# First mixer, last phase: outputs with channels on partitions, head norm by sums over partitions, scores in 64-row pairs

## The chip, the cores and the metric

The kernel runs on one core of a Trainium2 chip. The metric is device time in microseconds (us). Three runs of the kernel before took 4608.09, 4599.14 and 4606.88 us, so the median is 4606.88 us. The engines are named as in the profile: PE is TensorE (PEld its weight loads), DVE is VectorE, ACT is ScalarE, POOL is GpSimd, SP is SyncE, which here issues most of the DMAs.

## The reference

The program is a stack of four pairs of a mixer and a feed-forward part over 8 sequences of 512 tokens and 256 channels. The change lies in the first mixer alone, a gated delta rule with 4 heads of 64 channels. Cut to what matters, with `F` the gated sum of three causal filters of the values and a direct term, and `g` a gate of the head's path, which the kernel multiplies into the queries ahead of time:

```python
def step(S, inp):                       # one chunk of tokens of one head
    q_i, k_i, u_i, w_i = inp
    attn = where(causal, q_i @ k_i.T, 0.0)
    u_adj = u_i - w_i @ S
    o_i = q_i @ S + attn @ u_adj
    return S + k_i.T @ u_adj, o_i
o = g * delta_rule(q, k, v, beta) + F   # 64 channels per head
o = o * rsqrt(mean(o * o, -1) + 1e-5)   # norm over the 64 channels of a head
y = (o * norm_w) @ Wo.T                 # then a layer norm, added to x
```

The reference scans over chunks of 32 tokens; the kernel works with chunks of 128, which gives the same result.

## The kernel before

The first mixer, `l0_attn` (from L275), has three parts. The first makes queries, keys and values of each of the 8 sequences ("batches" below), their products and the inverses of the 64x64 triangles. The second (the filters, L511 to L640) makes the filter term with Toeplitz matrices: L610 multiplies in pairs of 64 output rows, `pf`, with every eighth element of `toep` as the moving operand. Both leave their results in DRAM. The third, from L644, is the phase that the change touches. It loads everything back per batch and runs the recurrence, the outputs, the head norm and the projection.

`loads(b)` (L671) issues the loads of one batch on SP's queue, in the order TT (two halves of the transposed inverse, L677), T1 (two blocks of 32 columns of the inverse, L682), TS (L686 and L689), keys, queries, PQ, V and F (L704). POOL then scales the queries (L707). The loads of a batch are issued when the batch before it begins, except that those of the first two stand at the start.

`back(b, ...)` (L710) is a generator. It first joins 64x64 inverses into 128x128 ones: `pW` (L719, 32x32 products of T1 and TT), `pX` (L728 and L731), `pU` and `pV` (L743 and L751, 64 output rows). Then it takes four chunks `n` of 128 tokens. For every second chunk it makes the scores of two chunks: ACT copies the two heads of a channel pair into a tile QP with zeros in the other half (L766), PE multiplies the keys with it over all 128 rows and 256 columns (`pa`, L773), DVE masks (L778). For each chunk: `pk` transposes the keys (L784), `pr` is keys times state (L791), R = V - pr (DVE, L795), `pu` (L799), u (DVE, L803), `pS` (L809), the new state (DVE, L816 or L818), and the outputs `po`: the filter term times the identity (L823), queries times state (L826), scores times u (L828), one sum in PSUM with tokens on partitions. ACT copies it (L832) and squares it (L834), DVE sums the squares (L835). After the four chunks: the reciprocal root by a shift and three Newton steps on DVE (L94 to L96, of 16 values per partition), the scaling on POOL (L841), eight transposes to channels on partitions (`poT`, L847), two ACT copies (L850), and the projection `py` (L193) with the closing norm (`stats`, L99; ACT scales, L177; POOL adds to X, L182).

Two batches are interleaved by the loop at the end of `l0_attn`: one generator step of each in turn, a new batch when fewer than two are live and the last has made 8 steps. A planner then orders the instructions of each engine by costs and dependences, so that PE's order differs from that of the program. PSUM tiles of the tag `mm` have 3 buffers, `seq` 3 and `st` 2. An fp32 product appears as two records on PE in the trace, a transpose as one.

Of the kernel before, what the change touches and what calls it, by code (L numbers as in the profile page):

```python
# [19 lines left out]
P = 128  # L20
NB = 8
L = 512
NT = 4
# [251 lines left out]
def l0_attn(K):  # L275
# [6 lines left out]
    with ExitStack() as es:  # L282
# [17 lines left out]
        def window(t, offset, *ap):  # L300
            a = t[0:1, 0:1]
            return bass.AP(tensor=a.tensor, offset=a.offset + offset, ap=[list(x) for x in ap])
# [350 lines left out]
        QPs, Us = [], []  # L653
        T1s = [p1.tile([P, NT, H, 32], F32, name=f"T1{i}") for i in range(2)]
        W21s = [p1.tile([P, NT, H, 32], F32, name=f"W21{i}") for i in range(2)]
        for i in range(2):
            t = p1.tile([P, 2, 2, 2, P], F32, name=f"QP{i}")
            nc.gpsimd.memset(t, 0.0)
            QPs.append(t)
            t = p1.tile([P, 2, H, 64], F32, name=f"U{i}")  # L660
            nc.gpsimd.memset(t, 0.0)
            Us.append(t)
# [8 lines left out]
        def loads(b):  # L671
# [9 lines left out]
            for r in range(2):  # L681
                nc.sync.dma_start(  # L682
                    out=T1s[b % 2][64 * r:64 * r + 32].rearrange("p n h t -> p (n h) t"),
                    in_=window(t_d, (b * 32 + r * 16) * 4096,
                               (64, 32), (4096, NT * H), (1, 32)))
# [24 lines left out]
        def back(b, TT, TS, qT, kT, V, F):  # L710
# [6 lines left out]
            for n, h in heads:  # L717
                for r in range(2):
                    nc.tensor.matmul(  # L719
                        ps[two[r], n, h, :], lhsT=TT[one[r], n, h, two[r]],  # L720
                        rhs=T1[one[r], n, h, :], start=True, stop=True)
# [34 lines left out]
            O = p1.tile([P, NT, H, 64], F32, tag="O", name=f"O{b}", bufs=2)  # L756
            os_ = p2.tile([P, NT, H], F32, tag="os", name=f"os{b}")
            S = None
            for n in range(NT):
                u_ = f"{b}_{n}"  # L760
                tok = slice(n * P, (n + 1) * P)
                if n % 2 == 0:
                    QP = QPs[b % 2]
                    for r in range(2):
                        half = slice(64 * r, 64 * r + 64)
                        nc.scalar.copy(  # L766
                            QP[half, :, :, r, :],
                            qT[half, :, n * P:(n + 2) * P].rearrange("p c (m t) -> p c m t", m=2))
                    att = p2.tile([P, 2, H, P], F32, tag="at", name="at" + u_)
                    for m in range(2):  # L770
                        pa = pmm.tile([P, H, P], F32, tag="mm", name=f"pa{m}_" + u_)
                        for c in range(2):
                            nc.tensor.matmul(  # L773
                                pa[:, 2 * c:2 * c + 2, :].rearrange("p h t -> p (h t)"),
                                lhsT=kT[:, c, (n + m) * P:(n + m + 1) * P],
                                rhs=QP[:, c, m].rearrange("p r t -> p (r t)"),
                                start=True, stop=True)
                        nc.vector.tensor_tensor(  # L778
                            att[:, m], pa, K.up[:, None, :].to_broadcast([P, H, P]), ALU.mult)
# [40 lines left out]
                po = pseq.tile([P, H, 64], F32, tag="seq", name="po" + u_)  # L820
                for c in range(2):
                    pc = po[:, 2 * c:2 * c + 2, :].rearrange("p h d -> p (h d)")
                    nc.tensor.matmul(  # L823
                        pc, lhsT=F[:, c, tok], rhs=K.ident, start=(c == 0), stop=False)
                    if n > 0:
                        nc.tensor.matmul(pc, lhsT=qT[:, c, tok], rhs=S[:, c, :], start=False, stop=False)  # L826
                    for h in range(2 * c, 2 * c + 2):
                        nc.tensor.matmul(  # L828
                            po[:, h, :], lhsT=at[:, h, :], rhs=u[:, 64 * h:64 * h + 64],
                            start=False, stop=(h == H - 1))  # L830
                S = Sn
                nc.scalar.copy(O[:, n], po)  # L832
                oq = p2.tile([P, H, 64], F32, tag="oq", name="oq" + u_)
                nc.scalar.activation(oq, po, AF.Square)  # L834
                nc.vector.tensor_reduce(os_[:, n, :], oq, AX.X, ALU.add)  # L835
                yield

            nc.vector.tensor_scalar(os_, os_, 1.0 / 64, 1e-5, ALU.mult, ALU.add)
            ro = K.rsqrt(os_.rearrange("p n h -> p (n h)"), NT * H, "rms", p2)
            ro = ro.rearrange("p (n h) -> p n h", n=NT)  # L840
            nc.gpsimd.tensor_tensor(  # L841
                O, O, ro[:, :, :, None].to_broadcast([P, NT, H, 64]), ALU.mult)
            oT = p1.tile([P, 2, L], F32, tag="oT", name=f"oT{b}")
            for c in range(2):
                ps = pmm.tile([P, L], F32, tag="mm", name=f"poT{b}_{c}")
                for n in range(NT):
                    nc.tensor.transpose(  # L847
                        ps[:, n * P:(n + 1) * P],
                        O[:, n, 2 * c:2 * c + 2].rearrange("p h d -> p (h d)"), K.ident)
                nc.scalar.copy(oT[:, c, :], ps)  # L850
            K.project_out(b, [(oT[:, c, :], wo[:, c, :]) for c in range(2)], pmm, "mm", p1)


        ahead = {b: loads(b) for b in range(2)}
# [18 lines left out]

# [1738 lines left out]
```

## Time and profile before

| | |
|---|---|
| profiled execution, its own time | 4604.57 us |
| its span | 4602.9 us |
| median of three runs | 4606.88 us |
| mean granted PE clock | 0.926 |
| changed phase, first `pW` to the first product of the next part | 408.2 to 733.4 us |
| PE, busy in 408 to 733 | 273.4 of 325 us |
| DVE, ACT, POOL, busy in 408 to 733 | 145.0, 104.7, 56.2 us |

The span is cut into windows for the views below: each line of a window view has the busy time and number of instructions of each engine, the mean granted clock of PE, and the DMAs' share. In the views by line a group has its busy time, the mean duration of one in ns, and the idle time of its engine just ahead of it with what ended it. In the timeline a merged line has the start, the length from the first start to the last end, and the number of records.

### The profile page before, as it was taken

The page shows a single profiled execution, that of the slowest core. Times are in us where ns is not written, and L with a number is a line of the kernel's source. Part 1 is how long each engine was busy: PE and PEld are TensorE (multiplying, and loading weights), DVE is VectorE, ACT ScalarE, POOL GpSimd, SP SyncE. Part 2 cuts the span into 40 slices and gives each one's busy share as a digit, 9 for nine tenths or more (in the row PEclk, how much of TensorE's full clock was granted, in tenths as well). Part 3 has the DMA queues.
Part 4 walks back from the last instruction along what each step waited for, and adds up shares of the span by engine and source line. Part 5 has one row for each costly group of instructions (what it writes and reads, how often), then busy time and mean ns, then how long its engine had stood idle before and what let it go on. Part 6 is the DMA issues. An engine that isn't in the chain of part 4 may idle for free. (4 is left out here: it accounts for less than half of the span.)

```text
span 4602.9 us, 63430 instructions
## 1 busy us (share of the span) xinstructions
PE 3998.6 (87%) x21704; PEld 2678.3 (58%) x21704; DVE 2704.0 (59%) x7367; ACT 1984.7 (43%) x4096; POOL 2037.1 (44%) x2004
## 2 busy tenths in 40 slices
PE   8887888899998599789999987888888876799997
PEld 3434775555565389744455543556555545578884
DVE  7695546347657711145556533889888899731115
ACT  5512333344433333424444444677767656311112
POOL 0001111444433344344555412889888879223321
PEclk9898899999999899879999998989999986899999
DMA  4468430100000189700000001443333334237753
GB/s 120 132 200 231 101 72 15 48 5 11 5 7 16 46 212 251 192 5 6 10 6 6 1 23 48 122 127 128 120 122 127 122 108 138 93 124 227 233 182 112
DMA packets 393586, 443.42 MB, mean 96 GB/s; under 512 B 151693, under 2 KB 275711, under 8 KB 392751
## 3 DMA queue, kind: packets, MB, share of 16 engines
q1 hardware_dynamic: 365311, 390.70, 28.7%
q0 software_dynamic: 16272, 31.87, 2.5%
q10 hardware_dynamic: 11680, 16.80, 1.1%
q8 instruction: 172, 2.82, 0.3%
q14 instruction: 151, 1.24, 0.1%
HBM read 373.02 MB, written 66.26 MB: 95 GB/s over the span
## 5 line engine op out<-in xcount | busy, mean ns | idle before, releaser
L2027 POOL TENSOR_TENSOR h<-h,C 128x1024 f32<-128x1024 f32 x256 | 613.6, 2410 | 135.2 <-DVE h L2023 91.1
L2023 DVE TENSOR_TENSOR_SCAN h<-dA,dB 128x512 f32<-128x512 f32 x480 | 568.5, 1209 | 89.6 <-ACT dA L2011 73.3
L981 POOL TENSOR_SCALAR p<-p,rs 128x128 f32<-128x128 f32 (+3 forms) x256 | 275.7, 1085 | 420.7 <-DVE rs L980 263.1
L2011 ACT ACTIVATE dA<-dl,A 128x512 f32<-128x512 f32 x480 | 330.4, 690 | 174.1 <-DVE h L2023 173.3
L1547 DVE CUSTOM_DVE_ANT_0 junk<-S,mask 128x256 f32<-128x256 f32 (+3 forms) x512 | 249.7, 488 | 194.9 <-PE S L1541 156.3
L2040 PE MATMUL y<-C,h 128*128 128x128 f32 x2048 | 298.3, 297 | 68.0 <-POOL h L2027 67.9
L2040 PEld LDWEIGHTS y<-C,h 128*128 128x128 f32 x2048 | 263.4, 155 | 155.2 <-POOL h L2027 98.6
L1575 ACT ACTIVATE PT<-T 128x128 f32<-128x128 f32 (+3 forms) x512 | 198.1, 435 | 279.2 <-PE T L1570 268.3
L1541 PE MATMUL S<-KZ,QT 64*128 64x512 f32 (+3 forms) x1024 | 259.7, 489 | 23.5 <-DVE mx L1547 23.3
L2239 PE MATMUL gb<-xbT,w_b 128*128 128x256 f32 (+1 forms) x1472 | 255.3, 332 | 1.0 <-ACT ts L2443 0.6
L2239 PEld LDWEIGHTS gb<-xbT,w_b 128*128 128x128 f32 x1472 | 230.2, 191 | 23.1 <-ACT ts L2443 0.8
L2245 DVE TENSOR_TENSOR hTb<-sb,gb 128x512 f32<-128x512 f32 x71 | 48.8, 687 | 325.4 <-PE gb L2239 325.4
L2006 POOL TENSOR_TENSOR dB<-du,B 128x1024 f32<-128x1024 f32 x96 | 234.0, 2438 | 0.1
L1825 PE MATMUL pf<-fT,w_l_ffn 128*128 128x512 f32 x384 | 210.3, 687 | 26.2 <-ACT fT L1819 10.4
L1570 PE MATMUL T<-QT,KZ 64*128 64x384 f32 (+3 forms) x1024 | 217.1, 465 | 2.9 <-ACT PT L1575 2.5
L2006 DVE TENSOR_TENSOR dB<-du,pb 128x1024 f32<-128x1024 f32 x160 | 191.2, 1195 | 23.2 <-ACT pb L2004 21.3
L1315 ACT ACTIVATE hT<-h,w_l_ffn 128x128 f32<-128x128 f32 x384 | 109.5, 368 | 198.0 <-PE h L1310 198.0
L182 POOL TENSOR_TENSOR X<-X,yn 128x256 f32<-128x256 f32 (+1 forms) x56 | 79.3, 1434 | 260.2 <-ACT yn L177 230.2
L1310 PE MATMUL h<-xgT,w 128*128 128x128 f32 x1536 | 185.2, 279 | 0.0
L1541 PEld LDWEIGHTS S<-KZ,QT 64*128 64x128 f32 x1024 | 116.6, 192 | 114.0 <-issue 58.7
L979 ACT ACTIVATE p<-p,nm 128x128 f32<-128x128 f32 (+3 forms) x256 | 143.5, 561 | 81.1 <-DVE nm L975 73.1
L1578 POOL TENSOR_SCALAR_AFFINE_SELECT PT<-PT 128x512 f32<-128x512 f32 x128 | 81.3, 635 | 219.4 <-ACT PT L1575 206.5
(579 smaller groups left out, 9191.3 us busy)
## 6 DMA issues: line engine op xcount, KB each, us to landing
w_b<-l3f_w SPq DMA_DIRECT2D x138, 512.0 KB
C<-xdd SPq DMA_DIRECT2D x256, 256.0 KB
B<-xdd SPq DMA_DIRECT2D x256, 256.0 KB
w<-l1f_w SPq DMA_DIRECT2D x48, 1024.0 KB
w<-l1f_w SPq DMA_DIRECT2D x48, 256.0 KB
toep<-l0fd SPq DMA_DIRECT2D x32, 320.0 KB
X<-x SPq DMA_DIRECT2D x16, 512.0 KB
toep<-l0fd SPq DMA_DIRECT2D x32, 256.0 KB
```

What stands on the lines that cost most here:

```text
L981: nc.gpsimd.tensor_scalar(p[:, 0:n], p[:, 0:n], rs, None, ALU.mult)
L1541: nc.tensor.matmul(ps[:, 0:n], lhsT=QT[half, qt * P:n], rhs=KZ[half, j % 2, 0:n], start=True, stop=True)
L1547: nc.vector.tensor_tensor_reduce(out=junk[:, 0:n], in0=ps[:, 0:n], in1=mask[:, L - n:L], scale=1.0, scalar=-3.0e38, op0=ALU.add, op1=ALU.m ...
L1570: nc.tensor.matmul(ps[:, 0:n], lhsT=KZ[half, j % 2, kt * P:(kt + 1) * P], rhs=QT[half, kt * P:L], start=True, stop=True)
L1575: nc.scalar.activation(PT[:, j, :], ps[:, 0:n], AF.Exp)
L1825: nc.tensor.matmul(ps, lhsT=gu[:, k, j * 768 + c * P:j * 768 + (c + 1) * P], rhs=R[b]["fT"][:, k, :], start=(k == 0), stop=(k == 1))
L2006: on.tensor_tensor(dBs[k], R[b]["du", h], B[:, None, :].to_broadcast([P, 2, L]), ALU.mult)
L2011: nc.scalar.activation(dA, R[b]["dl", h][:, c, :], AF.Exp, scale=A[:, 2 * h + c, n:n + 1])
L2023: nc.vector.tensor_tensor_scan(hs[k][:, c, :], dA, dBs[k][:, c, :], 0.0, ALU.mult, ALU.add)
L2027: nc.gpsimd.tensor_tensor(hs[k], hs[k], row_C.pop(k)[:, None, :].to_broadcast([P, 2, L]), ALU.mult)
L2040: nc.tensor.matmul(R[b]["y", h][q // 2][:, q % 2, c * P:(c + 1) * P], lhsT=t[:, c, q * P:(q + 1) * P], rhs=K.ident, is_transpose=True, sta ...
L2239: nc.tensor.matmul(ps[:, q, :], lhsT=ww[:, k, (c + q) * P:(c + q + 1) * P], rhs=xT[:, k, :], start=(k == 0), stop=(k == 1))
```

## The change

Outputs are made transposed. `po` has channels on partitions (two chunks of 128 channels) and tokens along the row: queries times state with the state as the stationary operand, and scores times u as products with 64 output rows, the two heads of a chunk one above the other. The filter term, which lies in DRAM with channels on partitions already, is added by DVE when it takes `po` out of PSUM. ACT squares the sum. After the four chunks a product with a block matrix of 1/64 (`ones2`, `pss`) gives each channel its head's mean square; ACT makes the reciprocal root from Ln and Exp, DVE makes one Newton step from it, and POOL and DVE scale. The copies, the transposes and the row sums of before are gone. The end of a batch has two steps more in the generator.

The scores are made without QP: keys and queries of a head are multiplied over its 64 rows, for the two heads of a channel pair in turn, into two PSUM tiles. DVE masks each.

`pW` reads the first block of the inverse from TS, so that only one block of T1 is loaded.

The closing norm of the batches takes the branch with Ln and Exp in `stats` (L108) for this phase, and their table is loaded ahead of the phase.

```diff
--- before.py
+++ after.py
@@ -650,13 +650,15 @@
             t = p1.tile([P, NT, H, P], F32, name=f"TT{i}")
             nc.gpsimd.memset(t[64:128, :, :, 0:64], 0.0)
             TTs.append(t)
-        QPs, Us = [], []
+        Us = []
+        ones2 = p1.tile([P, P], F32, name="ones2")
+        nc.gpsimd.memset(ones2, 0.0)
+        for r in range(2):
+            half = slice(64 * r, 64 * r + 64)
+            nc.gpsimd.memset(ones2[half, half], 1.0 / 64)
         T1s = [p1.tile([P, NT, H, 32], F32, name=f"T1{i}") for i in range(2)]
         W21s = [p1.tile([P, NT, H, 32], F32, name=f"W21{i}") for i in range(2)]
         for i in range(2):
-            t = p1.tile([P, 2, 2, 2, P], F32, name=f"QP{i}")
-            nc.gpsimd.memset(t, 0.0)
-            QPs.append(t)
             t = p1.tile([P, 2, H, 64], F32, name=f"U{i}")
             nc.gpsimd.memset(t, 0.0)
             Us.append(t)
@@ -678,11 +680,9 @@
                     out=TT[half, :, :, half].rearrange("p n h t -> p (n h) t"),
                     in_=window(tt_d, (b * 32 + r * 16) * 4096,
                                (64, 64), (4096, NT * H), (1, 64)))
-            for r in range(2):
-                nc.sync.dma_start(
-                    out=T1s[b % 2][64 * r:64 * r + 32].rearrange("p n h t -> p (n h) t"),
-                    in_=window(t_d, (b * 32 + r * 16) * 4096,
-                               (64, 32), (4096, NT * H), (1, 32)))
+            nc.sync.dma_start(
+                out=T1s[b % 2][64:96].rearrange("p n h t -> p (n h) t"),
+                in_=window(t_d, (b * 32 + 16) * 4096, (64, 32), (4096, NT * H), (1, 32)))
             nc.sync.dma_start(
                 out=TS[0:64].rearrange("p n h t -> p (n h) t"),
                 in_=window(t_d, b * 32 * 4096, (64, 64), (4096, NT * H), (1, 64)))
@@ -718,7 +718,7 @@
                 for r in range(2):
                     nc.tensor.matmul(
                         ps[two[r], n, h, :], lhsT=TT[one[r], n, h, two[r]],
-                        rhs=T1[one[r], n, h, :], start=True, stop=True)
+                        rhs=(T1 if r else TS)[one[r], n, h, 0:32], start=True, stop=True)
             nc.scalar.copy(W21[two[0]], ps[two[0]])
             nc.vector.tensor_copy(W21[two[1]], ps[two[1]])
             yield
@@ -753,30 +753,28 @@
                             rhs=U[:, n, h, :], start=True, stop=True)
                 nc.scalar.mul(TT[0:64, ns, :, 64:128], ps, -1.0)
                 yield
-            O = p1.tile([P, NT, H, 64], F32, tag="O", name=f"O{b}", bufs=2)
-            os_ = p2.tile([P, NT, H], F32, tag="os", name=f"os{b}")
+            oT = p1.tile([P, 2, L], F32, tag="oT", name=f"oT{b}", bufs=2)
+            sq = p1.tile([P, 2, L], F32, tag="sq", name=f"sq{b}", bufs=2)
             S = None
             for n in range(NT):
                 u_ = f"{b}_{n}"
                 tok = slice(n * P, (n + 1) * P)
                 if n % 2 == 0:
-                    QP = QPs[b % 2]
+                    att = p2.tile([P, 2, H, P], F32, tag="at", name="at" + u_)
+                    pss = [pmm.tile([P, 2, 2, P], F32, tag="mm", name=f"pa{r}_" + u_)
+                           for r in range(2)]
+                    for m in range(2):
+                        to = slice((n + m) * P, (n + m + 1) * P)
+                        for c in range(2):
+                            for r in range(2):
+                                half = slice(64 * r, 64 * r + 64)
+                                nc.tensor.matmul(
+                                    pss[r][:, m, c, :], lhsT=kT[half, c, to],
+                                    rhs=qT[half, c, to], start=True, stop=True)
                     for r in range(2):
-                        half = slice(64 * r, 64 * r + 64)
-                        nc.scalar.copy(
-                            QP[half, :, :, r, :],
-                            qT[half, :, n * P:(n + 2) * P].rearrange("p c (m t) -> p c m t", m=2))
-                    att = p2.tile([P, 2, H, P], F32, tag="at", name="at" + u_)
-                    for m in range(2):
-                        pa = pmm.tile([P, H, P], F32, tag="mm", name=f"pa{m}_" + u_)
-                        for c in range(2):
-                            nc.tensor.matmul(
-                                pa[:, 2 * c:2 * c + 2, :].rearrange("p h t -> p (h t)"),
-                                lhsT=kT[:, c, (n + m) * P:(n + m + 1) * P],
-                                rhs=QP[:, c, m].rearrange("p r t -> p (r t)"),
-                                start=True, stop=True)
                         nc.vector.tensor_tensor(
-                            att[:, m], pa, K.up[:, None, :].to_broadcast([P, H, P]), ALU.mult)
+                            att[:, :, r::2, :], pss[r],
+                            K.up[:, None, None, :].to_broadcast([P, 2, 2, P]), ALU.mult)
                 at = att[:, n % 2]
                 if n < NT - 1:
                     pk = pmm.tile([P, D], F32, tag="mm", name="pk" + u_)
@@ -817,40 +815,41 @@
                         else:
                             nc.vector.tensor_tensor(
                                 Sn[half, :, half], S[half, :, half], pS[half, :, half], ALU.add)
-                po = pseq.tile([P, H, 64], F32, tag="seq", name="po" + u_)
+                po = pseq.tile([P, 2, P], F32, tag="seq", name="po" + u_)
                 for c in range(2):
-                    pc = po[:, 2 * c:2 * c + 2, :].rearrange("p h d -> p (h d)")
-                    nc.tensor.matmul(
-                        pc, lhsT=F[:, c, tok], rhs=K.ident, start=(c == 0), stop=False)
                     if n > 0:
-                        nc.tensor.matmul(pc, lhsT=qT[:, c, tok], rhs=S[:, c, :], start=False, stop=False)
-                    for h in range(2 * c, 2 * c + 2):
                         nc.tensor.matmul(
-                            po[:, h, :], lhsT=at[:, h, :], rhs=u[:, 64 * h:64 * h + 64],
-                            start=False, stop=(h == H - 1))
+                            po[:, c, :], lhsT=S[:, c, :], rhs=qT[:, c, tok], start=True, stop=False)
+                    for r in range(2):
+                        h = 2 * c + r
+                        nc.tensor.matmul(
+                            po[64 * r:64 * r + 64, c, :], lhsT=u[:, 64 * h:64 * h + 64],
+                            rhs=at[:, h, :], start=(n == 0), stop=True)
                 S = Sn
-                nc.scalar.copy(O[:, n], po)
-                oq = p2.tile([P, H, 64], F32, tag="oq", name="oq" + u_)
-                nc.scalar.activation(oq, po, AF.Square)
-                nc.vector.tensor_reduce(os_[:, n, :], oq, AX.X, ALU.add)
+                nc.vector.tensor_tensor(oT[:, :, tok], F[:, :, tok], po, ALU.add)
+                nc.scalar.activation(sq[:, :, tok], oT[:, :, tok], AF.Square)
                 yield
 
-            nc.vector.tensor_scalar(os_, os_, 1.0 / 64, 1e-5, ALU.mult, ALU.add)
-            ro = K.rsqrt(os_.rearrange("p n h -> p (n h)"), NT * H, "rms", p2)
-            ro = ro.rearrange("p (n h) -> p n h", n=NT)
-            nc.gpsimd.tensor_tensor(
-                O, O, ro[:, :, :, None].to_broadcast([P, NT, H, 64]), ALU.mult)
-            oT = p1.tile([P, 2, L], F32, tag="oT", name=f"oT{b}")
+            ro = p1.tile([P, 2, L], F32, tag="ro", name=f"ro{b}")
             for c in range(2):
-                ps = pmm.tile([P, L], F32, tag="mm", name=f"poT{b}_{c}")
-                for n in range(NT):
-                    nc.tensor.transpose(
-                        ps[:, n * P:(n + 1) * P],
-                        O[:, n, 2 * c:2 * c + 2].rearrange("p h d -> p (h d)"), K.ident)
-                nc.scalar.copy(oT[:, c, :], ps)
+                ps = pmm.tile([P, L], F32, tag="mm", name=f"pss{b}_{c}")
+                nc.tensor.matmul(ps, lhsT=ones2, rhs=sq[:, c, :], start=True, stop=True)
+                nc.scalar.activation(sq[:, c, :], ps, AF.Identity, bias=K.eps)
+                nc.scalar.activation(ro[:, c, :], sq[:, c, :], AF.Ln)
+            yield
+            for c in range(2):
+                nc.scalar.activation(ro[:, c, :], ro[:, c, :], AF.Exp, scale=-0.5)
+                t, y, o = sq[:, c, :], ro[:, c, :], oT[:, c, :]
+                nc.gpsimd.tensor_tensor(o, o, y, ALU.mult)
+                nc.vector.tensor_tensor(t, t, y, ALU.mult)
+                nc.vector.scalar_tensor_tensor(t, t, -0.5, y, ALU.mult, ALU.mult)
+                nc.vector.scalar_tensor_tensor(o, t, 1.5, o, ALU.add, ALU.mult)
+            yield
             K.project_out(b, [(oT[:, c, :], wo[:, c, :]) for c in range(2)], pmm, "mm", p1)
 
 
+        K.log_exp_tables()
+        K.log_exp = True
         ahead = {b: loads(b) for b in range(2)}
         live, done, begun, steps = [back(0, *ahead[0])], 0, 1, 0
         while live:
@@ -870,7 +869,7 @@
                     K.load_x(K.i["x"], range(HALF, NB))
                 if begun < NB:
                     ahead[begun] = loads(begun)
-
+        K.log_exp = False
 
 
 def l0_ffn(K):
```

## The prediction

> **What bounds the kernel now.** I read the page's busy times first, then cut the changed phase (408 to 733 us) into windows, then asked for its groups by shape, and last for the timeline and for the waits of PE and SP. The page:
>
> ```profile
> PE 3998.6 (87%) x21704; PEld 2678.3 (58%) x21704; DVE 2704.0 (59%) x7367; ACT 1984.7 (43%) x4096; POOL 2037.1 (44%) x2004
> ```
>
> The windows of the phase (engines in the order PE, PEld, DVE, ACT, POOL; then the granted clock):
>
> ```profile
> 408.00:433.00 25.00, 20.17 (x260) 18.20 (x260) 3.46 (x6) 7.08 (x13) 3.62 (x3) 0.53 0.96 218
> 555.00:630.00 75.00, 66.30 (x777) 58.63 (x772) 37.31 (x141) 27.53 (x58) 15.00 (x8) 0.91 0.49 102
> 630.00:705.00 75.00, 66.30 (x773) 58.92 (x772) 35.22 (x124) 25.06 (x54) 10.81 (x5) 0.91 0.09 22
> 705.00:733.00 28.00, 14.44 (x79) 11.58 (x77) 12.83 (x61) 6.28 (x15) 4.25 (x2) 0.85 0.15 53
> ```
>
> Two batches take 75 us in the steady part, and PE is busy in 66.3 of them; DVE fills half, ACT a third. So PE sets the pace, at an unsteady clock, and the price of the change is PE's time plus what PE waits for. At both ends of the phase one batch is alone and its chain sets the pace. The groups that the change removes or recasts, in the phase:
>
> ```profile
> L773 PE MATMUL pa<-QP,bk 128*128 128x256 f32 x128 | 44.7, 494 | 7.6 <-DVE W L723 3.6 <-DVE at L778 3.3 <-ACT QP L766 0.7
> L828 PE MATMUL po<-u,at 128*128 128x64 f32 x256 | 37.1, 269 | 0.1
> L823 PE MATMUL po<-C,bf 128*128 128x128 f32 x128 | 28.7, 307 | 0.0
> L847 PE MATMUL poT<-C,O 128*128 128x128 f32 x64 | 10.4, 314 | 11.9 <-POOL O L841 11.9
> ```
>
> Their durations overlap in the pipeline, so I price by starts. In the timeline at full clock, the start of each merged line less that of the one before is what a group costs PE; the other parts show products of 64 rows (`pkk`) and of 64 output rows (`pf`):
>
> ```profile
> 574.58 1.99 PE L773 MATMUL pa<-QP,bk 128*128 128x256 f32 x8
> 576.41 0.38 PE L784 MATMUL pk<-C,bk 128*128 128x128 f32 x2
> ...
> 577.25 0.44 PE L823 MATMUL po<-C,bf 128*128 128x128 f32 x2
> 577.52 0.39 PE L826 MATMUL po<-state,bq 128*128 128x128 f32 x2
> 577.75 0.56 PE L828 MATMUL po<-u,at 128*128 128x64 f32 x4
> 578.14 0.66 PE L809 MATMUL pS<-u,kt 128*128 128x128 f32 x4
> ```
> ```profile
> 42.71 0.27 PE L473 MATMUL pvw<-C,vT 128*128 128x128 f32 x1
> 42.92 1.60 PE L486 MATMUL pkk<-kT 64*128 64x128 f32 x22
> 44.45 0.33 PE L146 MATMUL pxT<-C,xn 128*128 128x128 f32 x1
> ```
> ```profile
> 386.28 2.54 PE L610 MATMUL pf<-toep,Vw 128*64 128x256 f32 x9
> ```
>
> **The change on PE,** over the 8 batches, at full clock.
> - Filter term: 64 products (two records each) go, 0.25 us each (0.27 here, 0.22 at other places): -16.0. DVE's add takes the place of the row sum, both at 0.42 us (L795's row against L835's): no cost.
> - Scores: 16 groups of eight records at 1.83 us (574.58 to 576.41) are 29.3. After: 128 products of 64 rows. `pkk`, whose two halves alternate, has 21 steps in 1.33 us, 0.063 per record; halves that do not alternate start 0.112 apart. In the built order of the new kernel 75 of the 128 alternate and 53 do not: 75 x 0.126 + 53 x 0.224 = 21.3. So -8.0.
> - Transposes: 64 at 0.109, -7.0. In their place 16 products of 512 columns, two records of 0.43 each (the spacing of the projections, L435): +13.7.
> - Scores times u: 32 groups of two pairs at 0.40 (577.75 to 578.14) are 25.6. After: 128 products with 64 output rows and 128 columns. Here the rows disagree. `pf` is the nearest in form: eight steps in 1.90 us, 0.237 per record of 256 columns, 0.118 for 128, so 30.3 and a loss of 4.7. `pkk` is the nearest in how the operand is read (one run of 128): 0.063 per record, 16.1, and a gain of 9.5. I take the second, with 14 of the products alone in the built order (+0.8): -8.7. My reason: the records of `pf` start two at a time (0.03, then 0.43 apart), as those of `pkk` do (0.007, then 0.105), so the two tiles run together, and what doubles their time is then likely its operand of every eighth element.
> - Changes of tile shape: 42.71 to 42.92 is 0.21 where two full records stand 0.11 apart, and 44.25 to 44.45 again; 0.093 each. The built order has 70 such changes before and 204 after: +12.5.
>
> Sum: -16.0 - 8.0 - 7.0 + 13.7 - 8.7 + 12.5 = -13.5 at full clock. The mean clock of the phase is 0.877, so -15.4 (from -0.1, if `pf` is the row, to -16).
>
> [...] No run here shows a column pair with an unbroken operand. [...]
>
> **Waits of PE.** Gone: 6.1 us behind POOL (`poT`, waits of PE between 433 and 716) and, of the scores' waits for W and QP (3.6 and 0.7), half: -8.1. New, from the built order: `pss` of every second batch has only `pr` (0.45) ahead of it while DVE adds (0.42) and ACT squares (0.39): 0.6 x 4 = 2.4. `py` needs the first scaled half: ACT's Identity, Ln, Identity, Exp (4 x 0.59, by the copy `oT` of 512 elements), DVE's multiply, the other half's multiply and two more steps (4 x 0.68, by L621), 5.1 in all; PE meanwhile has 3.5 to 3.9: 1.35 x 7 = 9.5. In four batches R of the other batch is queued on DVE behind the multiply that waits for Exp, and `pu` for R: 0.35 x 4 = 1.4. Net +5.2 (0 to +12). DVE's own load hardly changes: per batch 13 small steps of the root and 10 of `stats` go (0.2 each), six of 0.68 come. ACT loses QP, O and oT copies (5.1 us per batch) and gains six of 0.59 and four small ones. POOL has 2 x 1.2 in place of 1.9. All beside PE.
>
> **The start.** `pW` now needs TS:
>
> ```profile
> 401.46 3.04 SPq L682 DMA_DIRECT2D T<-l0t  x2
> 408.04 0.58 SPq L686 DMA_DIRECT2D TS<-l0t  x1
> 408.22 2.10 PE L719 MATMUL pW<-T,TT 32*32 32x32 f32 x64 [10.54 <-DMA T<-l0t]
> ```
>
> TS's issue waited until 408.04 for a store of the filters (3.4 us by SP's waits), and the built kernel has the same waits on it. T1 landed 3.7 us after its issue; TS would land at 411.3 to 412.3. Everything of batch 0 follows: +3.1 (0 if the store is done sooner, +4). In later batches TS is there a batch ahead, and the T1 load that is gone was hidden.
>
> **The end.** The last batch is alone: 715.6 to 733.4. Its norm takes as long as before (first `py` 6.6 us after the last `po` against 7.6, the second half 2 us later), `stats` is shorter by some 1 us: -1 (-2 to +2). Two table loads of ACT (1.28 us as at the kernel's start) stand where ACT idles; +1.3 if the one for Tanh does not.
>
> **The clock.**
>
> ```profile
> 554.17:557.59 3.42, 2.01 (x69) 1.55 (x68) 2.68 (x13) 1.51 (x3) 0.00 (x0) 1.00 0.80 196
> 557.59:561.00 3.41, 2.63 (x6) 1.64 (x6) 2.20 (x11) 0.57 (x2) 0.00 (x0) 0.50 0.02 6
> 561.00:564.41 3.41, 3.41 (x22) 2.81 (x24) 0.69 (x1) 1.73 (x5) 1.67 (x1) 0.50 0.00 0
> 564.41:567.82 3.41, 2.51 (x107) 2.33 (x105) 2.33 (x7) 2.12 (x5) 0.68 (x1) 1.00 0.04 7
> ```
>
> After a window with `pW` and a gap of 1.4 us the clock is halved for two windows, once per batch, at 3.4 us of PE's time. [...]
>
> **Sum:** -15.4 + 5.2 + 3.1 - 1 = -8.1 for the parts, and -2 more because `pa`, over a third of whose records ran at half clock, is worth more than the mean: -10. On the profiled 4604.6 that is 4594.6; the median is 2.3 above it, so 4597 against 4606.9.
>
> **Rivals.**
> - Column pairs do not run together (for: `pf` is the only such row; against: its starts): 9.5 + 4.7 over 0.877 is +16, so 4613.
> - The clock, the one that ends slower: with fewer full-array records a window is thinner, and half-row records may count half. Each further half-clock window costs 1.7 us of PE's time. Six such windows in the 325 us take the gain away; two more per batch (16 x 1.7 = 27) give 4624. For: dips already come at 1.4 us of idling. Against: the dense `pu`, `py`, `pss`.
> - The dips go, because the scores no longer wait for QP beside `pW`: six of them, -20, 4577.
> - The change does not do what it says in part: 53 of 128 scores already run unpaired by the planner's order; were all unpaired, +7, 4604.
>
> **How the numbers follow.** 0.2% is 9.2 us, about what a measurement can tell. Forecast (own range 4585 to 4608) 0.42, of which a third lies within 0.2%; dips gone 0.13, faster; column pairs 0.15, of which 0.10 within; unpaired scores or longer waits 0.08, within 0.2%; the clock 0.22, slower. Faster 0.28 + 0.13 = 0.41; same 0.14 + 0.10 + 0.08 = 0.32; slower 0.05 + 0.22 = 0.27. The range runs from the dips' case to the clock's: 4576 to 4626.
>
> **What would show it.** `po` with u: records 0.06 apart means pairs, 0.12 none. `pa` near 21 us in starts. `pss` waiting for ACT by 0.6, `py` for DVE by 1.3. First `pW` near 411. Clock of the steady windows at 0.91: above 0.95 the dips went, below 0.85 the rival won. I am wrong if PE's busy share in the steady windows falls without the two batches taking less than 75 us.

## The result, and where the time went

The changed kernel takes 4631.41 us (median of six runs, 4623.63 to 4633.80) against 4609.38 us before (six runs); the ratio is 1.0048, with a 95% interval of 1.0035 to 1.0061. The forecast was 4597. The profiled execution of the changed kernel has a span of 4632.1 us, 29.2 more than the one before; it is the slowest of its six, so its parts add up to more than the 22 us between the medians.

The changed phase now runs from 413.58 us (first `pW`) to 763.25 us (first `pm`). These are its windows, with the columns as before: busy time and instructions of PE, PEld, DVE, ACT and POOL, then the granted clock of PE.

```profile
413.50:433.00 19.50, 15.49 (x248) 14.48 (x248) 1.80 (x3) 4.09 (x7) 2.35 (x1) 0.50 0.95 234
555.00:630.00 75.00, 63.91 (x727) 51.99 (x726) 41.07 (x101) 20.96 (x45) 17.18 (x10) 0.82 0.45 98
630.00:705.00 75.00, 64.16 (x739) 51.09 (x740) 36.74 (x85) 25.02 (x51) 14.06 (x7) 0.86 0.20 50
705.00:763.00 58.00, 41.43 (x177) 28.77 (x176) 25.65 (x59) 14.61 (x31) 9.24 (x5) 0.72 0.05 18
```

In the steady part the clock fell from 0.91 to 0.82 and 0.86, PE is busy for two microseconds in 75 less, and two batches take 82 us (every second batch's first `pW` is at 490.22, 572.14 and 654.29). The falling busy share, and the 0.82 in the first of these windows, are signs that the prediction had named for its own failure.

The phase can be cut into three parts that add up. "Work" is PE's busy time weighted with the granted clock, so what it would be at full clock (the records of `py` of the changed kernel start 0.216 us apart at full clock and 0.427 at half). The granted clock is taken from the trace's own record of it. "Clock" is busy time less work, what the half clock cost. "Idle" is the rest. All are of the stretch from the first `pW` to the first `pm` of the profiled execution, in us; "half" is the time in which the granted clock was 0.5.

| kernel | phase | work | clock | idle | half |
|---|---|---|---|---|---|
| before | 325.2 | 239.8 | 33.5 | 51.8 | 79.4 |
| changed | 349.7 | 230.4 | 57.7 | 61.6 | 134.6 |

The work fell by 9.4 us, as the change promised. The clock took 24.2 and idle time 9.8. With a start that is 5.4 us later this is the 29 us.

Where PE idles, and which group pays, is in the groups of the phase (busy, mean ns of one, idle time ahead and what ended it), first `py` of the kernel before, then PE's and DVE's groups of the changed kernel:

```profile
L193 PE MATMUL py<-w_l_attn,oT 128*128 128x256 f32 x128 | 31.5, 401 | 0.5 <-ACT oT L850 0.5
```

```profile
L193 PE MATMUL py<-w_l_attn,oT 128*128 128x256 f32 x128 | 49.2, 553 | 29.6 <-DVE oT L846 29.6
L771 PE MATMUL pa<-bq,bk 64*128 64x128 f32 x256 | 33.4, 328 | 4.0 <-ACT yn L177 2.2 <-DVE at L775 1.8
L825 PE MATMUL po<-at,u 128*64 128x128 f32 x256 | 33.1, 327 | 1.2 <-DVE u L801 0.7 <-DVE at L775 0.4
L836 PE MATMUL pss<-sq,ones 128*128 128x512 f32 x32 | 17.7, 679 | 3.5 <-ACT sq L830 2.3 <-DVE at L775 1.2
```
```profile
L844 DVE TENSOR_TENSOR sq<-sq,ro 128x512 f32<-128x512 f32 x16 | 19.5, 1219 | 7.9 <-ACT ro L841 7.9
L845 DVE SCALAR_TENSOR_TENSOR sq<-sq,ro 128x512 f32<-128x512 f32 x16 | 17.6, 1101 | 0.0
L846 DVE SCALAR_TENSOR_TENSOR oT<-sq,oT 128x512 f32<-128x512 f32 x16 | 15.2, 950 | 0.2
```

`py`, the projection, itself unchanged, waits 29.6 us for the norm and then takes 49.2 instead of 31.5 us. The three DVE steps of the norm, forecast at 0.68 us each, take 0.95 to 1.22 on average. The timeline of one batch shows why they are long (start, length, engine); it is headed by two lines from the first batch:

```profile
472.70 2.78 POOL L707 TENSOR_TENSOR bq<-bq,PQ 128x1024 f32<-128x1024 f32 x1
473.20 2.82 DVE L846 SCALAR_TENSOR_TENSOR oT<-sq,oT 128x512 f32<-128x512 f32 x1
```
```profile
593.40 0.69 DVE L844 TENSOR_TENSOR sq<-sq,ro 128x512 f32<-128x512 f32 x1 [0.25 <-ACT ro L841]
593.45 3.44 POOL L843 TENSOR_TENSOR oT<-oT,ro 128x512 f32<-128x512 f32 x2 [11.04 <-ACT ro L841]
...
594.34 1.43 DVE L845 SCALAR_TENSOR_TENSOR sq<-sq,ro 128x512 f32<-128x512 f32 x1
...
595.70 1.74 DVE L844 TENSOR_TENSOR sq<-sq,ro 128x512 f32<-128x512 f32 x1
597.36 0.68 DVE L846 SCALAR_TENSOR_TENSOR oT<-sq,oT 128x512 f32<-128x512 f32 x1
597.97 0.68 DVE L845 SCALAR_TENSOR_TENSOR sq<-sq,ro 128x512 f32<-128x512 f32 x1
...
598.10 2.08 PE L193 MATMUL py<-w_l_attn,oT 128*128 128x256 f32 x4 [2.23 <-DVE oT L846]
```

Ahead of `py` stand the first half's steps L844, L845 and L846, and between them the other half's L844. POOL's two multiplies stand from 593.45 to 596.89. A DVE step that starts beside one of them does not end until 0.55 us after it (595.70 + 1.74 is 597.44); one that starts before POOL, or when POOL is done, takes 0.68. In the first two batches L846 is held up as well, for 2.82 us, by POOL's scaling of the queries (L707). This holds for all 48 of these steps in the phase: 18 began while POOL ran, took 1.43 to 2.82 us and ended 0.55 us after POOL's instruction; the other 30 took 0.68 or 0.69. And the windows of 3.41 us around it show what follows:

```profile
590.22:593.63 3.41, 3.15 (x20) 1.88 (x18) 1.23 (x4) 2.67 (x5) 0.18 (x1) 1.00 1.35 179
593.63:597.05 3.42, 1.38 (x10) 1.19 (x10) 3.42 (x4) 1.09 (x3) 3.26 (x2) 1.00 1.03 321
597.05:600.46 3.41, 2.37 (x6) 1.63 (x6) 2.53 (x5) 0.00 (x0) 0.00 (x0) 0.50 0.78 176
600.46:603.87 3.41, 3.41 (x12) 2.58 (x12) 0.00 (x0) 0.37 (x1) 0.00 (x0) 0.50 0.00 0
```

In the window from 593.63 PE is busy for 1.38 us (`pu` waits 1.01 us for R, which DVE makes only after L844, and at the end `py` waits for the norm), and in the two that follow its clock is 0.50: just then the dense `py` runs. After 433 us the clock dropped nine times before the change and sixteen times after it. Of the sixteen, eight come after a window in which `py` waits for the norm (the last of these waits, from 746.81 to 752.77, begins in a stretch that is at half clock already; the clock is back for the window from 747.24, in which PE does nothing, and halved again after it), one at the very end, where the next part waits for the last norm, and seven after windows with `pX`, with a wait of `pu`, or full of `pa`.

### The profile page after: what moved, and what is told of

It is laid out like the page before. It is cut to its first block, busy times and chain, and to the rows that moved or that the text cites. A ratio compares the mean times of both kernels' runs of the same rounds, so it can differ in the third digit from the quotient of the medians.

```text
span 4632.1 us, 63233 instructions
## 1 busy us (share of the span) xinstructions
PE 4020.1 (87%) x21672; PEld 2670.7 (58%) x21672; DVE 2724.2 (59%) x7231; ACT 1984.8 (43%) x4082; POOL 2049.3 (44%) x2013
## 3 DMA queue, kind: packets, MB, share of 16 engines
q8 instruction: 172, 2.82, 0.3%
## 5 line engine op out<-in xcount | busy, mean ns | idle before, releaser
L980 POOL TENSOR_SCALAR p<-p,rs 128x128 f32<-128x128 f32 (+3 forms) x256 | 275.8, 1085 | 417.0 <-DVE rs L979 260.8
L1540 PE MATMUL S<-KZ,QT 64*128 64x512 f32 (+3 forms) x1024 | 260.9, 495 | 22.6 <-DVE mx L1546 22.4
L2238 PEld LDWEIGHTS gb<-xbT,w_b 128*128 128x128 f32 x1472 | 230.4, 191 | 22.8 <-ACT ts L2442 0.8
L182 POOL TENSOR_TENSOR X<-X,yn 128x256 f32<-128x256 f32 (+1 forms) x56 | 79.4, 1436 | 274.7 <-ACT yn L177 244.7
L1309 PEld LDWEIGHTS h<-xgT,w 128*128 128x128 f32 x1536 | 178.0, 194 | 0.0
```

The lines of the kernel that those rows point to most:

```text
L980: nc.gpsimd.tensor_scalar(p[:, 0:n], p[:, 0:n], rs, None, ALU.mult)
L1309: nc.tensor.matmul(ph[:, j, :], lhsT=w1[:, s, c, m * P:(m + 1) * P], rhs=xgT[:, c, :], start=(c == 0), stop=(c == 1))
L1540: nc.tensor.matmul(ps[:, 0:n], lhsT=QT[half, qt * P:n], rhs=KZ[half, j % 2, 0:n], start=True, stop=True)
L2238: nc.tensor.matmul(ps[:, q, :], lhsT=ww[:, k, (c + q) * P:(c + q + 1) * P], rhs=xT[:, k, :], start=(k == 0), stop=(k == 1))
```

## The experiments

Two theories were set against each other. **A:** the norm's chain on DVE is late, since DVE stands while POOL multiplies; `py` waits, the window goes thin, and the clock is halved for `py`. **B:** the products of 64 rows or 64 columns fill only half of the 128 by 128 of the others (64*128 and 128*64 in the profile, against 128*128), and that by itself thins the windows. The table holds every kernel's phase, cut as above, and its time as a ratio to runs of the kernel before that were made beside it. Kernels of different rows are best compared by these ratios.

| kernel | phase | work | clock | idle | half | median us | ratio (95%) |
|---|---|---|---|---|---|---|---|
| changed | 349.7 | 230.4 | 57.7 | 61.6 | 134.6 | 4631.4 | 1.0048 (1.0035, 1.0061) |
| e1_dve | 311.0 | 233.0 | 31.4 | 46.7 | 72.8 | 4603.0 | 0.9994 (0.9984, 1.0004) |
| e2_lean | 275.1 | 228.3 | 22.3 | 24.5 | 50.1 | 4552.6 | 0.9877 (0.9860, 0.9893) |
| e3_full | 335.5 | 228.7 | 41.2 | 65.6 | 106.8 | 4618.6 | 1.0028 (1.0018, 1.0037) |
| e8_fill | 335.5 | 253.0 | 36.4 | 46.1 | 82.9 | 4614.7 | 1.0016 (1.0006, 1.0026) |
| e4_pairs | 326.8 | 236.0 | 41.9 | 48.9 | 98.1 | 4610.3 | 1.0018 (1.0008, 1.0028) |
| e10_lean_full | 275.3 | 230.7 | 19.0 | 25.7 | 43.6 | 4555.4 | 0.9888 (0.9874, 0.9903) |
| e6_lean_t1 | 275.8 | 228.9 | 17.1 | 29.8 | 40.6 | 4560.0 | 0.9901 (0.9888, 0.9913) |
| e11_lean_pool | 276.7 | 227.4 | 18.8 | 30.4 | 44.6 | 4555.3 | 0.9890 (0.9875, 0.9904) |

The five columns of the phase are of one profiled execution each, which can lie some way off the kernel's median (10 us below it for e1_dve, 11 above for e2_lean). Differences of a few us in them show little.

**e1_dve: POOL's multiply on DVE.**

```diff
-                nc.gpsimd.tensor_tensor(o, o, y, ALU.mult)
+                nc.vector.tensor_tensor(o, o, y, ALU.mult)
```

> The changed kernel, with POOL's multiply of the norm (L843) put on DVE. In the trace of the changed kernel DVE's two-operand steps of the norm take 0.69 us where POOL is idle, and 1.4 to 1.75 us where POOL's multiply runs beside them, ending 0.55 us after POOL's end. Theory A (the clock falls because py waits for the norm, and the norm is slow because DVE stands while POOL multiplies): all of DVE's steps take 0.69, PE's wait for the scaled outputs falls from 29.6 us to 10 to 20, some of the eight dips of the clock at py go, and the time is 4595 to 4618 (changed kernel 4631, before 4609). Theory B (the clock falls because products of 64 rows or columns fill the array half): the half-clock time in the phase stays at 125 us or more (135 in the changed kernel, 79 before), and the time is 4616 to 4628. If POOL has no part in DVE's length, L844 to L846 keep a mean over 0.9 us.

DVE has a step more per half, and each of its steps is shorter (DVE's groups of this kernel):

```profile
L843 DVE TENSOR_TENSOR oT<-oT,ro 128x512 f32<-128x512 f32 x16 | 11.0, 688 | 7.5 <-ACT ro L841 7.5
L844 DVE TENSOR_TENSOR sq<-sq,ro 128x512 f32<-128x512 f32 x16 | 10.9, 684 | 0.0
L845 DVE SCALAR_TENSOR_TENSOR sq<-sq,ro 128x512 f32<-128x512 f32 x16 | 10.9, 683 | 0.0
L846 DVE SCALAR_TENSOR_TENSOR oT<-sq,oT 128x512 f32<-128x512 f32 x16 | 10.9, 683 | 0.1
```
```profile
L193 PE MATMUL py<-w_l_attn,oT 128*128 128x256 f32 x128 | 42.7, 493 | 14.2 <-DVE oT L846 14.2
```

Four steps now take DVE 43.7 us where three took 52.3. The wait of `py` fell from 29.6 to 14.2 us, the half-clock time from 134.6 to 72.8, and the time by 25 us by the ratios. It is no faster and no slower than the kernel before. Theory A's numbers, all of them; B wanted 125 us or more at half clock. Two reservations: with other costs the planner also set part of `py` of every second batch a little later, behind `pW`, so not all of the 15 us of wait need be DVE's shorter steps; and the profiled execution lies 10 us below the median, so the usual half-clock time may be somewhat longer.

**e2_lean: no Newton step, and Ln straight from PSUM.**

```diff
-                nc.scalar.activation(sq[:, c, :], ps, AF.Identity, bias=K.eps)
-                nc.scalar.activation(ro[:, c, :], sq[:, c, :], AF.Ln)
+                nc.scalar.activation(ro[:, c, :], ps, AF.Ln, bias=K.eps)
...
-                nc.gpsimd.tensor_tensor(o, o, y, ALU.mult)
-                nc.vector.tensor_tensor(t, t, y, ALU.mult)
-                nc.vector.scalar_tensor_tensor(t, t, -0.5, y, ALU.mult, ALU.mult)
-                nc.vector.scalar_tensor_tensor(o, t, 1.5, o, ALU.add, ALU.mult)
+                nc.vector.tensor_tensor(o, o, y, ALU.mult)
```

> The changed kernel without the Newton step of the norm: Ln reads the product of the squares straight from PSUM, Exp, and one multiply on DVE; ACT's Identity, POOL's multiply and three DVE steps of each half go (the root is left as Exp gives it). From the end of pss the first half then needs Ln 0.62, Exp 0.62 and a multiply of 0.69, 1.9 us, while PE has 1.1 to 2.1 us of other work. Theory A (waits of py, and the clock that follows them): PE's wait for the scaled outputs falls from 29.6 us to under 8, the dips at py go (about 16 half-clock windows of 3.4 us less, 27 us of PE time), and the time is 4570 to 4594. Theory B (thin products): the half-clock time stays over 120 us, only the wait itself is won, 4600 to 4612.

The wait of `py` is all but gone, and two batches fill PE (the group, then a window of this kernel):

```profile
L193 PE MATMUL py<-w_l_attn,oT 128*128 128x256 f32 x128 | 31.7, 390 | 2.6 <-DVE oT L842 2.6
```
```profile
555.00:630.00 75.00, 71.96 (x894) 59.44 (x894) 36.40 (x102) 27.95 (x57) 10.32 (x5) 0.93 0.43 95
```

It beats both kernels, by 54 us the one before, and it went below theory A's own range (4570 to 4594): not only the dips at `py` went, the half-clock time is under that of the kernel before. PE is busy in 72 of 75 us where it was in 66, and few windows are thin any more. With a short norm the changed kernel is thus a good 1% faster than the kernel before; the late norm had eaten that. No run gave the kernel before a shorter norm, so how much of this belongs to the change and how much to the Newton step left out is not shown.

**e3_full: the scores by full rows.**

```diff
                         for c in range(2):
-                            for r in range(2):
-                                half = slice(64 * r, 64 * r + 64)
-                                nc.tensor.matmul(
-                                    pss[r][:, m, c, :], lhsT=kT[half, c, to],
-                                    rhs=qT[half, c, to], start=True, stop=True)
+                            nc.tensor.matmul(
+                                pss[m][:, c, :, :].rearrange("p m t -> p (m t)"),
+                                lhsT=kT[:, c, to], rhs=qT[:, c, n * P:(n + 2) * P],
+                                start=True, stop=True)
```

> The changed kernel with scores by products of all 128 rows and 256 columns, eight records per pair of chunks as in the kernel before; the zero padding is left out, so the two heads of a channel pair are added up in the scores. Theory A: the eight dips at py stay; PE has 8 us more work at full clock; at most the four dips that begin in windows full of pa (528, 607, 689 and 727 us) go, 14 us: 4624 to 4642, half-clock time over 105 us. Theory B: the windows are full again, half-clock time falls to about 80 us as before the change, and the time is 4605 to 4618.

4618.6 us lies between the two. The wait of `py` even rose (36.4 us), as A has it, and yet the half-clock time fell by 28 us. It is above B's range by a hair, and below A's; the half-clock time (106.8) is just over A's bound of 105 and far from B's 80. So B is not wrong, only the smaller part of the time (9 us by the ratios, against 25 in e1_dve): some of the sixteen drops need the half-filled `pa`. (Of the four windows that the expectation calls full of `pa`, the one at 607 has 96 records of `pX` and none of `pa`.) The two causes work together: what the half clock cost fell by 16.5 us here and by 26.3 in e1_dve, more in sum than the 24.2 that it had risen. The planner also set PE's work in another order here, to which part of the longer waits may belong. And the full rows did not cost the 8 us that were expected: between starts, at full clock, `pa` went from 25.0 to 29.0 us, while the whole work fell by 1.7.

**e8_fill: more work, in the place of the wait.**

```diff
                 nc.scalar.activation(ro[:, c, :], sq[:, c, :], AF.Ln)
+                if c == 1:
+                    dm = pmm.tile([P, L], F32, tag="mm", name=f"dm{b}")
+                    for k in range(4):
+                        nc.tensor.matmul(dm, lhsT=ones2, rhs=qT[:, k % 2, :], start=True, stop=True)
```

> The changed kernel with more work: after the product of the squares of each batch, four products of all rows and columns by 512 that nothing reads (3.4 us per batch at full clock, 27 in all). Theory A with the clock as the larger part: they fill the time in which PE waits for the norm, the windows at py are no longer thin, most of the 16 half-clock windows there go, and in spite of 27 us more work the time falls, to 4600 to 4622. Theory B, or a wait that costs only its own length: the dips stay or move, and the time is 4630 to 4655.

PE has 22.6 us more work, and the kernel is 15 us faster (ratios 1.0016 against 1.0048): idle time 15.5 less, and what the half clock costs 21.3 less. With products that nothing reads it was faster, and its time at half clock fell from 134.6 to 82.9 us. The wait of `py` is still 20.8 us, since the products run right after `pss` and, in every second batch, other work (`pS`, `po`) is pushed behind the first `py`; drops remain there.

**e4_pairs: the kernel before, with the scores in 64-row pairs alone.** The edit is the part of the change that puts `kT[half]` and `qT[half]` in the place of QP.

> The kernel before, with the scores alone changed to products of 64 rows, for two heads in turn; outputs and norm as before. pa costs PE 5.5 us less at full clock by starts (30.5 to 25.0), and PE's waits for QP and for W ahead of pa (4.3 us) are gone or halved. Theory A: 4596 to 4604 (before 4606 to 4609). Theory B: windows of 16 half-row records halve the clock in four or more batches, and the time is 4609 to 4625.

```profile
408.30:735.10 326.80, 277.88 (x3217) 250.08 (x3217) 144.12 (x539) 86.88 (x192) 54.91 (x29) 0.85 0.43 97
```

Its whole phase in one window: the clock is 0.85, where it was 0.88. Work fell by 3.9 us and idle time by 2.9, as the pairs promise; the half clock took 8.4 back, and the time rose by 0.18%. The clock dropped nine times after 433 us, as often as before, but seven of the drops lasted 10.2 us or more, where one had. In four of the seven the window after which the clock had not come back was mostly of half-filled `pa`, in three of `pX`. Here B decides: this part of the change, by itself, is a loss. (The profiled execution lies 4 us below the median, and its phase shows only 1.6 of the 8 us.)

**e10_lean_full: e2_lean with the scores of e3_full.** The edit is the sum of both.

> The kernel without the Newton step (4553 us, 0.9877 of the kernel before), with scores by products of all 128 rows and 256 columns, eight records per pair of chunks; zero padding is left out, so the two heads of a channel pair are added up in the scores. Between starts, at full clock, pa cost 25 us in that kernel and 29 with full rows. Theory A (only waits thin the windows): 4 to 5 us more, 4555 to 4562. Theory B, as far as it is left (the windows at 567 and 632 us, with 16 records of pa, were thin enough to halve the clock): two to four half-clock windows less for each, 7 to 14 us, and 4542 to 4551.

4555.4 us, 0.9888 against 0.9877, intervals overlapping: no difference can be told. It is at the lower edge of A's range and above B's. By the trace the pairs save 2.4 us of work and cost 3.3 of clock. Where PE waits little, no run shows that the pairs help or hurt.

**e6_lean_t1: e2_lean with both blocks of T1.** The two places of the diff that concern T1 and TS are undone.

> The kernel without the Newton step, with both blocks of T1 loaded again, so that pW need not wait for TS. If the start moves the whole phase (first pW at 413.6 us in the changed kernel, 411.3 without the Newton step, 408.2 before): 3 to 5 us less, 4546 to 4552. If the loads only queue one behind the other on SP, no difference: 4551 to 4556.

In the trace `pW` starts 0.2 us after TS's issue, and in e2_lean 3.9 us after it; from TS's issue to the first `pm` it is 276.0 us against 279.0. The median shows none of that (4560.0, 0.9901, above both ranges): differences of a few us between kernels timed at different times are not to be had. The start of the phase itself moves by several us from one execution to the next (TS's issue stood at 407.4 to 410.9 in these profiles, and it waits for a store of the part before).

**e11_lean_pool: e2_lean with the multiply on POOL.**

```diff
-                nc.vector.tensor_tensor(o, o, y, ALU.mult)
+                nc.gpsimd.tensor_tensor(o, o, y, ALU.mult)
```

> The kernel without the Newton step, with the one multiply that is left on POOL (1.74 us) instead of DVE (0.69). It prices a wait: py's first half is 1.05 us later, the second 2.1. Theory A: the waits for the scaled outputs rise from 2.6 us to 8 to 20, each beyond some 1.5 us brings a dip of 3.4 us, and the time is 4562 to 4590. If a wait costs its length alone: 4556 to 4570, with a half-clock time in the phase as without the change (53 us).

4555.3 us, no slower, and just below both ranges. The wait of `py` rose to 7.4 us, below the expected 8, with none over 1.35 us, and the half-clock time was even lower. POOL on the chain does little harm here, as the norm leaves DVE nothing to do beside it, and it is quicker itself (POOL's group of this kernel):

```profile
L842 POOL TENSOR_TENSOR oT<-oT,ro 128x512 f32<-128x512 f32 x16 | 20.0, 1266 | 78.8 <-ACT ro L840 78.8
```

1.27 us, the 1.2 that the prediction gave it, and 1.74 in the changed kernel, where DVE's steps stood beside it, as DVE's took 1.43 us or more when POOL had begun first: each holds up the other. So the expectation, which took 1.74 for it, was too high by that much. The seven waits of 1.0 us or less brought no drop. The longest, 1.35 us (the last batch, at 681.26) with another of 0.30, stands in the first of these windows, and the clock fell after it:

```profile
679.63:683.04 3.41, 1.76 (x7) 1.00 (x7) 0.00 (x0) 1.50 (x3) 2.53 (x2) 1.00 0.00 0
683.04:686.45 3.41, 3.41 (x10) 2.70 (x9) 0.98 (x4) 0.00 (x0) 0.00 (x0) 0.50 0.00 0
```

One such drop does not give the price of longer waits.

## Why the prediction was wrong

**PE's own work: right in sign, 9.4 instead of 13.5.** By starts, at full clock: the filter term 18.2 less (forecast 16.0), the transposes 7.8 less (7.0), `pss` 14.6 (13.7), the scores 5.5 less (8.0), scores times u 4.3 less (8.7). The question of the column pairs came out as chosen: in a run of eight, the records of `po` start at 592.004 and 592.010, 592.164 and 592.170, 592.273 and 592.279, two at a time, 0.109 from pair to pair, that is 0.055 per record. So it was not by its shape that `pf` was slow; that its operand is the reason was not tried. The other groups, at the changes of shape, cost 11.8 more (forecast 12.5). What is missing is at the changes too, within the scores and the products with u: the first pair of such a run takes mostly 0.15 to 0.16 in `po` and 0.21 or more in `pa` instead of 0.11, and after it the first full record is 0.2 away, and the second 0.16 to 0.21 from that; a change cost more than the single 0.093.

**The waits: the step that failed.** The prediction said: DVE's multiply, the other half's multiply and two more steps, "4 x 0.68, by L621", 5.1 us in all against PE's 3.5 to 3.9, so 9.5 us for `py` in seven batches. In those seven it was 23.7 (29.6 with the last batch, which the prediction had counted with the end). ACT's steps (0.62 to 0.68 us each, forecast 0.59) and PE's cover were about as said, and `pss` waited 2.3 for ACT (2.4). The waits that were to go went: `poT`'s, and those of the scores fell from 7.6 to 4.0 (the 8.1 forecast is 8.2 or 8.3 by its own terms, which changes nothing); `pu`'s for R hardly moved, from 7.3 to 7.5, where 1.4 more were forecast. But the row of L621 is of steps that had POOL idle beside them, and the change puts a POOL multiply exactly beside these steps; the forecast put the loads of DVE, ACT and POOL down as "All beside PE" and gave POOL's effect on DVE no term. The trace of before had shown this effect, in the same line:

```profile
345.28 4.07 POOL L360 TENSOR_SCALAR_AFFINE_SELECT X<-X 128x4096 f32<-128x4096 f32 x1 [84.57 <-DMA l0f<-s]
...
346.33 3.55 DVE L621 TENSOR_TENSOR s<-pr 128x512 f32<-128x512 f32 x1
```

One of the 32 L621 steps of the span (median 0.68 us) took 3.55 us, and ended 0.53 after POOL's. Asked for by its longest instead of its mean, the row would have said so. With DVE's steps at 0.68, 1.43, 1.74 and 0.68, 4.5 in the place of 2.7, the same sum of the prediction gives 3.2 us per batch, about what PE waited (3.4 in the mean of the seven: 2.2 to 3.2 in five, and 5.3 and 4.4 in the first two, where L707 held up a step more).

**The clock: without a term in the forecast, measured at 24.2 us.** The rival "the clock" had the size (27 us, 4624), the place (two more windows per batch) and its own condition, but its trigger was put down to thinner products, with "dense `py`" as evidence against it. It was mostly the reverse: the wait ahead of `py` is what thins the window in eight of the sixteen drops, and the dense `py` then runs at half clock; e3_full shows that the half-filled `pa` had a part in the rest. Between starts 83 of its 127 counted records ran at half clock, 9 of 127 before. The two errors were one: the wait of 9.5 us was split into pieces of 1.35, of which not every one need have dropped a window (in e11_lean_pool the one wait of 1.35 us did; before the change, of three waits of `poT` of 1.63 to 1.65 us, one); at 2.2 us and more, all eight did. The chances treated the longer waits (0.08) and the clock (0.22) as two cases, though the one brings about the other.

**Gap or thin window.** The prediction's row had a halving after a gap of 1.4 us, and in the runs shorter gaps went with one too: the clock was halved after the window from 593.63, where PE was busy for 1.38 of 3.42 us between pauses of 0.85 and 1.19, and after this one, in which PE never paused for longer than 0.8 us but ran 16 records of half the rows:

```profile
528.78:532.19 3.41, 2.62 (x22) 2.30 (x21) 1.47 (x3) 2.60 (x6) 1.30 (x1) 1.00 0.02 5
532.19:535.61 3.42, 3.42 (x22) 3.19 (x21) 2.35 (x7) 0.96 (x2) 1.06 (x1) 0.50 0.00 0
```

In this window of the kernel before, PE was busy for less and paused for longer (1.12 us), but all its 12 records were of 128 rows and columns (8 of `poT`, 4 of `py`), and the clock stayed at 1.00 in the next:

```profile
659.99:663.40 3.41, 2.05 (x12) 1.72 (x13) 0.42 (x1) 1.24 (x3) 1.06 (x1) 1.00 0.02 5
```

In this pair the busier window, with the half-filled products, was the one that the half clock followed. That such products count for less is a reading of this pair; no run shows it by itself. In every window full of `pa` that halved the clock PE waited too, if for 0.45 us only (the one ahead of 730.17); e4_pairs (0.18% slower) and e10_lean_full (no difference) bound what they cost.

**The start:** forecast 3.1 later; TS's issue to the first `pW` is 4.0 us where it was 0.2, and the rest of the 5.4 is an issue that itself came 1.6 us later. **The end:** forecast 1 us less; from the last `po` to the first `py` it was 11.1 us instead of 7.8, by the same steps of DVE and at half clock; from that `po` to the first `pm` it is 3.6 us more.

## What to carry to other kernels

When a step is moved to an engine, price it by rows in which the same neighbour was busy, and look at a row's longest beside its mean: two engines that are each half idle may still hold each other up (here a DVE step took 0.68 us, and 1.43 to 2.82 when POOL had begun first). When a change lengthens a chain that PE waits for, price the clock with the wait: here 9.8 us more idle time and half-filled products brought 24.2 us of clock, and it was paid by the dense products that followed. And when a good idea measures slower, look for the part that spoils it: without the Newton step and POOL's multiply the changed kernel is 1.2% faster than the kernel before.

## What the hardware showed that I had not expected

A kernel with 22.6 us more PE work ran 15 us faster, with 82.9 us at half clock in the place of 134.6: the products that nothing reads stood in part where PE had waited. The clock was halved after two windows in which no single pause was longer than 0.8 us, with 16 half-row records of `pa` in each (from 528.78 and 689.21). And a DVE step of 128 by 512 took 0.68 us, or 1.43 to 2.82, and in all 48 cases the longer time went with a POOL instruction that had begun before it.
